# Decoder layer and gated cross attention: work beside the last cross group in other steps, and the mask of its last two batches on VectorE

## The chip, the cores and the metric

One Trainium2 chip; the kernel runs on one of its cores. The metric is the device time of one execution in microseconds (us). A core has TensorE (PE in the profile; PEld is its weight loads), VectorE (DVE), ScalarE (ACT), GpSimd (POOL) and SyncE (SP), which here issues nearly all DMAs.

## The reference, cut to what matters

All is float32: 16 batches of 128 tokens with 512 features, 16 heads of 32.

```python
# L0: a decoder layer
x = x + attention(layernorm(x), itself, ltor_mask) @ w_ao + b_ao            # A: self attention
x = x + attention(layernorm(x), ctx, cross_mask) @ w_co + b_co             # B: cross attention
x = x + gelu(layernorm(x) @ w1 + b1) @ w2 + b2                              # C: MLP, 512 -> 2048 -> 512
# attention: scores = q k^T / sqrt(32); scores = scores * mask - 10000 * (1 - mask); softmax; @ v
# L1: gated cross attention (D)
a = layernorm(ctx); scores = (x Wq^T)(a Wk^T)^T * scale, -inf where masked; softmax; @ (a Wv^T)
x = x + tanh(gate) * out @ Wo^T
```

The cross mask has a 128x128 plane of its own for each batch, shared by the heads.

## The kernel before

**Groups and sections.** The tokens stay in SBUF as four groups of four batches. `attend` (from line 651) runs sections A0 to A3, then B0 to B3 (B3 is "the last cross group"), then the MLP (`mlp`) for all groups, then the gated sections D0 to D3.

**Units and steps.** A section has 16 steps. Step k belongs to the unit (batch k // 4, quarter m = k % 4); a unit holds four heads' scores of one batch, 128 x 512. Scores of unit 2_1 are those of batch 2, quarter 1. One step issues, in this order: the four `pT` DMAs of a pair of units (`receive_pair`, at odd k - 5); the score matmuls of a whole batch at m = 0 (`sc_B`); the *jobs* planned for this step; the output product of a finished batch (`mo_B`); the product with the values at m == 2 of the batch that is two batches old (`mix`, `av_B`); `turn_unit` of unit k - 3 (VectorE transpose, then the DMA `away_B` to DRAM); `norm_unit` of unit k - 2 (VectorE reciprocal, POOL multiply `s_B<-s_B,sum_B`); `least_unit` and `exp_unit` of unit k - 1 (VectorE minimum `mn_B<-s_B`, ScalarE's four exps); `scale_unit` of this batch's units (VectorE, PSUM scores times the mask plane into SBUF: unit 0 in the first step, 1 and 2 in the second, 3 in the third); `add_mask` of this unit (POOL: s + ma, `s_B<-s_B,mask`). The trailing steps 16 to 23 of the last section drain the pipeline and have jobs too.

**Order.** Every instruction is issued through `InOrder`, which keeps each engine in program order (so all instructions have line 50 in the profile, and tiles are told apart by name). An engine that waits holds back all that is queued behind it. This goes for SP's queue of DMAs too.

**Jobs beside the last cross group.** `beside_last_cross` (line 1585) makes the plan. It has:
- `gated_start` (line 1349): keys and values of the first gated group from normalised encoder tokens (`key_job`, `value_job`: 8 matmuls each, `mm_v`, then a ScalarE copy and a DMA `kept_v_D`).
- `mlp_start` (line 1004): LayerNorm of the first MLP group's tokens, their way through DRAM (`turned_C`), the four returned parts (`ml.part`, DMA `back_C<-turned_C`) and `chunk_back`, which on ScalarE applies the LayerNorm's scale and bias (`T_C<-back_C`).
- `loads`: the steps in which one 256 KB block of the first weight tiles is sent for. w1_0, w1_1 and w2_0 (which of the two matrices, and the number of the hidden block) have four blocks each.
- `at_`: the steps in which the MLP's generator goes on to its next `yield`.

**The MLP.** Its products go by a scheme with 7 half-size products instead of 8. It needs sums of weight quarters (`weight_sums`, line 981: t1 to t4, `t<-w`) and of token quarters (`token_sums`: `sx`). For hidden block n, `sums` gives the sums for w1 (`t1_n`) and for w2 (`t2_n`). Those of w1_0 run on POOL, one for each of the generator's steps; those of w2_n and w1_(n+1) wait in a list, `todo`, and run on VectorE:

```python
for _ in range(min(2, len(todo))):      # line 1244, after each of the 7 products r
    todo.popleft()()
```

Each of the four sums of a weight tile subtracts two quarters; the first needs the tile's blocks 0 and 1, the second blocks 2 and 3 and the first sum. The products `h_0_p` of a hidden block (PSUM, PE) are then added up in SBUF by VectorE (`h<-h,h`); ScalarE applies GELU. The product `h_n_p` of the first block uses three PSUM tags in turn, those of later blocks one bank, `mm0`, which also held the last product of the first block.

**D's mask.** The gated sections set `adds_only`. There, VectorE adds a mask to each head's scores and finds the minimum in one custom instruction (`tensor_tensor_reduce`, `s_D<-sc_D,gmask`, 128x128 each, four to a unit with an accumulator read behind each), straight from PSUM.

Of the kernel before, what the change touches and what calls it, by code (L numbers as in the profile page):

```python
# [19 lines left out]
Q = 32  # L20
# [33 lines left out]
def decoder_then_gated_cross_attention(ctx: ExitStack, tc: tile.TileContext, a: dict, out: bass.AP):  # L54
# [451 lines left out]
    class Section:  # L506
# [1 line left out]

        deferred, v_bias, at_end, adds_only = False, None, False, False

        def mixed_tile(self, b):
            return work.tile([P, KC, S], F32, tag="mT", name=f"mT_{self.name}_{b}", bufs=1)
# [22 lines left out]
    def by_head(t):  # L537
        return t.rearrange("p n c j -> p c n j")

    def scale_unit(bt, j):  # L540
        s = work.tile([P, NQ, KC, Q], F32, tag="s", name=f"s_{bt.name}_{j}", bufs=7)
        if bt.by_array:
            s = s.rearrange("p n c j -> p (n c j)").rearrange("p (c n j) -> p n c j", c=KC, n=NQ)
        bt.s[j] = s
        sc = bt.sc.pop(j).rearrange("p (c n k) -> p c n k", c=KC, n=NQ)
        if bt.sec.adds_only:
            bt.mn[j] = least_tile(bt, j)
            bt.sec.mask_and_least(by_head(s), sc, bt.b, bt.mn[j])
        else:
            bt.sec.scale_mask(by_head(s), sc, bt.b)  # L550
# [2 lines left out]
        return work.tile([P, KC], F32, tag="mn", name=f"mn_{bt.name}_{j}", bufs=6)  # L553

    def least_unit(bt, j):
        if not bt.sec.adds_only:
            bt.mn[j] = least_tile(bt, j)
            nc.vector.tensor_reduce(bt.mn[j], by_head(bt.s[j]), AX.XY, ALU.min)

# [91 lines left out]
    def attend(sections, ready, others, after=None):  # L651

        if not ready:
            sections[0].start(sections[1])
        units, batches = [], []
        projected = deque()  # L660

        def by_transfer(n):

            return min(n, (len(sections) * GB - 1) * GB) if ready else n

        def step(k, bt=None, jobs=(), ahead=None):

            m = k % GB
            pair = k - 5
            if pair % 2 and 0 <= pair < by_transfer(len(units)):  # L670
                receive_pair(*units[pair])
            if m == 0 and bt is not None:
                scores(bt)
            due()
            for job in jobs:
                job()
            if projected and (m == 0 or ready and bt is None):
                before = projected.popleft()
                if before.sec.deferred:
                    afterwards("act", lambda: before.sec.put_away(before))  # L680
                else:
                    out_project(before)
            done = k // GB - 2
            if ready and k == by_transfer(k) + 7:
                done = len(batches) - 1
                mix(batches[done])
                projected.append(batches[done])
            elif m == 2 and 0 <= done < len(batches) - ready:
                mix(batches[done])
                projected.append(batches[done])  # L690
            if ahead is not None:
                ahead.prepare(k % NS)
            if 0 <= k - 3 < len(units):
                (turn_unit if k - 3 < by_transfer(k) else turn_by_array)(*units[k - 3])
            def norm():
                if 0 <= k - 2 < len(units):
                    norm_unit(*units[k - 2])

            def exp():
                if 0 <= k - 1 < len(units):  # L700
                    least_unit(*units[k - 1])
                    exp_unit(*units[k - 1])


            for do in (exp, norm) if ready else (norm, exp):
                do()
            if bt is not None:
                for j in SCALED[m]:
                    scale_unit(bt, j)
                bt.sec.add_mask(by_head(bt.s[m]), bt.b)  # L710

        k = 0
        for i, sec in enumerate(sections):
            last = i + 1 == len(sections)
            jobs = others() if last else sections[i + 1].jobs()
            ahead = sections[i + 2] if i + 2 < len(sections) else after if i + 2 == len(sections) else None
            for b in range(GB):
                bt = Batch(sec, b)
                batches.append(bt)
                for m in range(GB):  # L720
                    units.append((bt, m))
                    step(k, bt, jobs.get(k % NS, ()), ahead)
                    k += 1
        while projected or k < len(units) + 2 * GB:
            step(k, jobs=jobs.get(k - len(units) + NS, ()))
            k += 1
# [14 lines left out]
    class SelfAttention(Section):  # L741
# [107 lines left out]
        def add_mask(self, s, b):  # L849
            nc.gpsimd.tensor_tensor(s, s, bcast_rows(ma1), ALU.add)  # L850

    def encoder_rows(g):
        return a["ctx_2048"][g * GB : (g + 1) * GB].rearrange("b s d -> (b s) d")

# [18 lines left out]
    class CrossAttention(Section):  # L873
# [95 lines left out]
        def scale_mask(self, s, sc, b):  # L969
            nc.vector.tensor_tensor(s, sc, bcast_rows(self.ms[:, b, :]), ALU.mult)  # L970

        def add_mask(self, s, b):
            nc.gpsimd.tensor_tensor(s, s, bcast_rows(self.ma[:, b, :]), ALU.add)

# [29 lines left out]
    def mlp_start(ml):  # L1004

        ml.pieces = deque()

        ml.b2 = load_row(a["L0_xattn_b2"], "b2_row")
        ml.db1 = cpool.tile([P, NF], F32, tag="db1", name="db1")
        for i in range(NI):  # L1010
            b1, c0 = columns["b1"]
            c0 += i * KC
            nc.vector.tensor_tensor(
                ml.db1[:, 2 * i : 2 * i + 2], b1[:, c0 + 2 : c0 + 4], b1[:, c0 : c0 + 2], ALU.subtract
            )

        def row_difference():
            ml.db2 = work.tile([P, H], F32, tag="row", name="db2_row", bufs=2)
            nc.vector.tensor_tensor(ml.db2[:, 0:HF], ml.b2[:, HF:H], ml.b2[:, 0:HF], ALU.subtract)

        ml.lnT = []
        def start():
            ml.lnT.append(act_tile("C0"))
            ml_begin(0)

        sends = [lambda b=b: ml_send(0, b) for b in range(GB)]
        back = [lambda k=k: chunk_back(ml.lnT[0][:, k], ml.back, k, "ln3_s", "ln3_b") for k in range(KC)]
        return (
            ([start, row_difference, lambda: ml_receive(0)], [0, 5, 7]), (sends, [0, 1, 2, 3]), (back, [12, 13, 14, 15]),
            ([lambda m=m: ml.part(m) for m in range(NQ)], [7, 9, 9, 11])  # L1030
        )

    def ml_begin(g):
# [8 lines left out]
    def mlp(ml, last_steps):  # L1042
# [143 lines left out]
        O_ORDER = (0, 1, 3, 5, 6, 2, 4)  # L1186
        w1, w2, right1, right2 = {}, {}, {}, {}

        w1[0], w1[1], w2[0] = load(0, 1), load(1, 1), load(0, 2)
        yield  # L1190

        right1[0], todo, _ = sums(0, 1, "kT", w1.pop(0), nc.gpsimd)
# [8 lines left out]
        for n in range(len(steps) + 1):  # L1201
# [35 lines left out]
            for r in range(7):  # L1237
                if n < len(steps):
                    p = H_ORDER[r]
                    hidden_product(n, p, sides[p], right1[n][p], h)  # L1240
                if before is not None:
                    p = O_ORDER[r]
                    out_product(n - 1, p, before[0][p], right2[n - 1][p], acc)
                for _ in range(min(2, len(todo))):
                    todo.popleft()()
                for do in at_[r]:
                    if do is not None:
                        do()
                if r == 1 and n + 1 < len(steps):
                    w2[n + 1] = load(n + 1, 2)  # L1250
                elif r == 2 and n + 2 < len(steps):
                    w1[n + 2] = load(n + 2, 1)
                last_steps(n, r)
                if n == 1 and r == 3:
                    for d, t in unkept:
                        nc.sync.dma_start(out=d, in_=t)
                yield
# [91 lines left out]
    def gated_start(first):  # L1349
# [12 lines left out]
        def keep_later(key, t, n, wait):  # L1362
# [4 lines left out]

        return (
            ([lambda c=c: key_job(c) for c in range(KC)], [1, 2, 3, 5]),
            ([lambda b=b: value_job(b) for b in range(GB)], [7, 9, 11, 13]),  # L1370
        )

    class GatedAttention(Section):
# [184 lines left out]
                ([lambda g=g, b=b: send(g, b) for g in range(3) for b in range(GB)], [8, 9, 10, 11, 13, 14, 15, 16, 19, 19, 19, 19]),  # L1558
            )

        adds_only = True

        def mask_and_least(self, s, sc, b, least):

            ma = self.ma[:, b, :].rearrange("p (n k) -> p n k", k=Q)
            for c in range(KC):
                nc.vector.tensor_tensor_reduce(
                    s[:, c], sc[:, c], ma, 1.0, LARGEST, ALU.add, ALU.min, least[:, c : c + 1]
                )

        def add_mask(self, s, b):
            pass
# [12 lines left out]
    def beside_last_cross():  # L1585
        flip[0], in_blocks[0] = 2, False
        def piece():
            due()
            next(in_mlp)

        at_ = [0, 8, 10, 12, 14, 15, 15, 16, 16, 17, 18, 19, 19, 20, 21, 21, 22, 23, 23]
        loads = [3, 5, 5, 7, 11, 11, 13, 13, 14, 15, 15, 16]
        return plan(
            *gated_start(first), *mlp_start(ml), *decoder[-1].tokens_again([1, 1, 3], (1, 0, 2)), ([piece] * len(at_), at_),
            ([lambda: ml.pieces.popleft()()] * len(loads), loads),
        )
# [95 lines left out]
```

## Time and profile before

| | |
|---|---|
| median of 3 runs | 1166.15 us (1164.99 to 1167.93) |
| profiled execution | 1167.72 us, span 1165.9 us |
| granted TensorE clock, mean | 0.997 |
| PE busy | 1132.2 us, 97% of the span |
| VectorE, ScalarE, POOL busy | 739.5, 605.8, 701.3 us |
| HBM traffic | 164 MB read, 94 MB written, 222 GB/s |

"Busy" is the time in which the engine has an instruction running; PEclk is the granted clock in tenths of full speed. In a line of a timeline stand: start in us from the span's start, duration in us, engine, line, operation, out<-in with buffer numbers left out, shape, count, and in brackets the idle time of the engine before it and what ended that. An "SPq" line is SP's issuing of a DMA. The last cross group runs to about 530 us, the MLP follows from there.

### The profile page before, as it was taken

Reading aid. Unit: us, or ns where it says so; the run is one execution under the profiler, and the core shown is the slowest. Engines: PE = TensorE matmul, PEld = TensorE weight load, DVE = VectorE, ACT = ScalarE, POOL = GpSimd, SP = SyncE. Lnnn points to the kernel's source line nnn. Section 1 sums busy time; section 2 is a strip of 40 time slices with the busy share of each in tenths; the row PEclk is TensorE's granted clock in tenths of the full one; section 3 lists DMA queues with packets and bytes.
Section 4 is the critical chain, followed back from the end, with each engine's and each line's share of the span. In section 5 each row is a group of like instructions: output and inputs, shape, how many; then the busy total and the mean of one; then the engine's idle time right before and its main releaser. Section 6 shows DMA issues by size and latency. Waiting matters only on the chain. (4 is left out here: it accounts for less than half of the span.)

```text
span 1165.9 us, 22021 instructions
## 1 busy us (share of the span) xinstructions
PE 1132.2 (97%) x7202; PEld 862.6 (74%) x7202; DVE 739.5 (63%) x1893; ACT 605.8 (52%) x2132; POOL 701.3 (60%) x636
## 2 busy tenths in 40 slices
PE   6999999999999999998999999999999999999998
PEld 5877777657575756545788888888888777787875
DVE  7678878797878876866654634443441238767763
ACT  2467667666666766765231233223222247787653
POOL 7698878688868675675233514443342268454973
PEclk9999999999999999998999999999999999999999
DMA  6598979999889879898797696696447817988874
GB/s 228 148 221 223 239 187 221 249 243 261 196 227 213 235 203 248 240 283 256 258 299 235 181 293 187 201 276 253 154 160 240 245 48 200 255 239 236 262 213 158
DMA packets 325121, 259.78 MB, mean 223 GB/s; under 512 B 83528, under 2 KB 280336, under 8 KB 320144
## 3 DMA queue, kind: packets, MB, share of 16 engines
q1 hardware_dynamic: 324968, 258.38, 78.1%
q8 instruction: 57, 0.93, 0.3%
q14 instruction: 56, 0.46, 0.1%
q10 hardware_dynamic: 40, 0.01, 0.0%
HBM read 163.94 MB, written 94.37 MB: 222 GB/s over the span
## 5 line engine op out<-in xcount | busy, mean ns | idle before, releaser
L50 DVE TENSOR_TENSOR h<-h,h 128x512 f32<-128x512 f32 x80 | 54.9, 686 | 113.4 <-PE h L50 113.4
L50 ACT ACTIVATE s_A<-s_A,mn_A 128x128 f32<-128x128 f32 x256 | 99.5, 394 | 51.2 <-issue 37.3
L50 ACT ACTIVATE s_B<-s_B,mn_B 128x128 f32<-128x128 f32 x256 | 99.5, 393 | 47.0 <-issue 32.7
L50 ACT ACTIVATE h<-h 128x512 f32<-128x512 f32 x64 | 40.3, 630 | 160.6 <-DVE h L50 160.6
L50 POOL TENSOR_TENSOR s_D<-s_D,sum_D 128x512 f32<-128x512 f32 x64 | 66.6, 1041 | 63.4 <-DVE sum_D L50 60.1
L50 ACT ACTIVATE s_D<-s_D,mn_D 128x128 f32<-128x128 f32 x256 | 99.2, 392 | 0.1
L50 POOL TENSOR_TENSOR s_B<-s_B,sum_B 128x512 f32<-128x512 f32 x64 | 67.0, 1046 | 49.9 <-DVE sum_B L50 44.4
L50 POOL TENSOR_TENSOR s_A<-s_A,sum_A 128x512 f32<-128x512 f32 x64 | 66.5, 1040 | 36.0 <-DVE sum_A L50 35.5
L50 POOL TENSOR_TENSOR s_A<-s_A,ma 128x512 f32<-128x512 f32 x64 | 81.7, 1277 | 5.4 <-DVE s_A L50 3.7
L50 POOL TENSOR_TENSOR s_B<-s_B,mask 128x512 f32<-128x512 f32 x64 | 81.3, 1271 | 2.1 <-DMA away_B<-s_B 0.4
L50 POOL TENSOR_TENSOR rstd_aD<-rstd_aD,mhalf 128x1 f32<-128x1 f32 x12 | 6.6, 550 | 114.6 <-DVE rstd_aD L50 101.1
L50 POOL TENSOR_TENSOR sh<-h 128x512 f32<-128x512 f32 x32 | 40.7, 1272 | 51.0 <-ACT h L50 43.0
L50 PE MATMUL mo_B<-w_co,mT_B 128*128 128x512 f32 x128 | 60.9, 620 | 1.5 <-ACT mT_B L50 1.5
L50 PE MATMUL h<-T_C,t 128*128 128x256 f32 x256 | 60.7, 380 | 1.3 <-DVE h L50 1.3
L50 PE MATMUL h<-T_C,w 128*128 128x256 f32 x256 | 61.0, 381 | 0.8 <-DVE h L50 0.8
L50 PE MATMUL h<-sx,t 128*128 128x256 f32 x256 | 60.6, 379 | 0.0
L50 PE MATMUL o<-w,h 128*128 128x256 f32 x256 | 60.5, 379 | 0.0
L50 PE MATMUL o<-t,h 128*128 128x256 f32 x256 | 60.5, 379 | 0.0
L50 PE MATMUL o<-t,sh 128*128 128x256 f32 x256 | 60.5, 379 | 0.0
L50 PE MATMUL mo_A<-w_ao,mT_A 128*128 128x512 f32 x128 | 59.1, 604 | 0.0
L50 DVE CUSTOM_DVE_ANT_0 s_D<-sc_D,gmask 128x128 f32<-128x128 f32 x256 | 57.0, 283 | 1.0 <-DMA turned_x<-x_D 0.8
L50 PE MATMUL mm_q_B<-T_B,w_cq 128*128 128x512 f32 x128 | 57.3, 595 | 0.0
(324 smaller groups left out, 2977.5 us busy)
## 6 DMA issues: line engine op xcount, KB each, us to landing
t<-kept SPq DMA_DIRECT2D x24, 1024.0 KB, 7.6
away_A<-s_A SPq DMA_DIRECT2D x64, 256.0 KB, 2.8
pT_A<-away_A SPq DMA_DIRECT2D x128, 128.0 KB, 3.0
away_B<-s_B SPq DMA_DIRECT2D x64, 256.0 KB, 4.5
pT_B<-away_B SPq DMA_DIRECT2D x128, 128.0 KB, 3.6
away_D<-s_D SPq DMA_DIRECT2D x60, 256.0 KB, 3.9
pT_D<-away_D SPq DMA_DIRECT2D x120, 128.0 KB, 3.1
w<-in_L_xattn_w_dram SPq DMA_DIRECT2D x24, 512.0 KB, 5.8
```

The costliest lines, as they stand in the source:

```text
L50: return lambda *args, **kw: self.tc.keep_in_program_order(call(*args, **kw))
```

## The change

Five edits, all beside or in the last cross group and the first MLP hidden block.

1. Returned parts of the first MLP group are sent for in steps 7, 7, 9, 9 (before 7, 9, 9, 11), and `chunk_back` runs in steps 12, 13, 14, 14 (before 12 to 15).
2. The gated group's last two value jobs move from steps 11 and 13 to 13 and 15.
3. POOL's four sums of w1_0 go to steps 10, 11, 12, 13 (before 8, 10, 12, 14); the weight blocks after the first four are sent for in steps 13 to 18 (before 11 to 16), and w2_0 is loaded ahead of w1_1.
4. In hidden block 0, VectorE's weight sums run one behind each of products 0 to 3 and two behind 4 and 5 (before two behind each of 0 to 3).
5. In group B3, batches 2 and 3 (8 units): after the scale, VectorE adds the mask and finds the minimum with four custom instructions a unit, as in D but on the scaled scores in SBUF. POOL's `add_mask` and VectorE's `tensor_reduce` of those units go. `adds_only` becomes `by_head_from`, the batch from which a section does this: 0 in D, 2 in B3, never elsewhere.

```diff
 def scale_unit(bt, j):
-        if bt.sec.adds_only:
+        if bt.b >= bt.sec.by_head_from:
             bt.mn[j] = least_tile(bt, j)
             bt.sec.mask_and_least(by_head(s), sc, bt.b, bt.mn[j])
         else:
             bt.sec.scale_mask(by_head(s), sc, bt.b)
 def least_unit(bt, j):
-        if not bt.sec.adds_only:
+        if bt.b < bt.sec.by_head_from:
             bt.mn[j] = least_tile(bt, j)
             nc.vector.tensor_reduce(bt.mn[j], by_head(bt.s[j]), AX.XY, ALU.min)
 # attend.step
-                bt.sec.add_mask(by_head(bt.s[m]), bt.b)
+                if bt.b < sec.by_head_from:
+                    bt.sec.add_mask(by_head(bt.s[m]), bt.b)
+    def mask_by_head(s, sc, ma, least):
+        ma = ma.rearrange("p (n k) -> p n k", k=Q)
+        for c in range(KC):
+            nc.vector.tensor_tensor_reduce(
+                s[:, c], sc[:, c], ma, 1.0, LARGEST, ALU.add, ALU.min, least[:, c : c + 1]
+            )
 # CrossAttention
+        by_head_from = property(lambda self: 2 if self.g == NG - 1 else GB)
+        def mask_and_least(self, s, sc, b, least):
+            self.scale_mask(s, sc, b)
+            mask_by_head(s, s, self.ma[:, b, :], least)
 # mlp_start
-            ([start, row_difference, lambda: ml_receive(0)], [0, 5, 7]), (sends, [0, 1, 2, 3]), (back, [12, 13, 14, 15]),
-            ([lambda m=m: ml.part(m) for m in range(NQ)], [7, 9, 9, 11])
+            ([start, row_difference, lambda: ml_receive(0)], [0, 5, 7]), (sends, [0, 1, 2, 3]), (back, [12, 13, 14, 14]),
+            ([lambda m=m: ml.part(m) for m in range(NQ)], [7, 7, 9, 9])
 # mlp
-        w1[0], w1[1], w2[0] = load(0, 1), load(1, 1), load(0, 2)
+        w1[0], w2[0], w1[1] = load(0, 1), load(0, 2), load(1, 1)
-                for _ in range(min(2, len(todo))):
+                for _ in range(min(1 if n == 0 and r < GB else 2, len(todo))):
 # gated_start
-            ([lambda b=b: value_job(b) for b in range(GB)], [7, 9, 11, 13]),
+            ([lambda b=b: value_job(b) for b in range(GB)], [7, 9, 13, 15]),
 # beside_last_cross
-        at_ = [0, 8, 10, 12, 14, 15, 15, 16, 16, 17, 18, 19, 19, 20, 21, 21, 22, 23, 23]
-        loads = [3, 5, 5, 7, 11, 11, 13, 13, 14, 15, 15, 16]
+        at_ = [0, 10, 11, 12, 13, 15, 15, 16, 16, 17, 18, 19, 19, 20, 21, 21, 22, 23, 23]
+        loads = [3, 5, 5, 7, 13, 14, 15, 16, 17, 17, 18, 18]
```

More of the change, by code (lines that the diff above doesn't have):

```diff
@@ L506, in decoder_then_gated_cross_attention @@
     class Section:
-        deferred, v_bias, at_end, adds_only = False, None, False, False
+        deferred, v_bias, at_end, by_head_from = False, None, False, GB
         def mixed_tile(self, b):
@@ L1559, in deferred_jobs @@
             )
-        adds_only = True
+        by_head_from = 0
         def mask_and_least(self, s, sc, b, least):
[L1565 to L1569, printed above, removed]
+            mask_by_head(s, sc, self.ma[:, b, :], least)
         def add_mask(self, s, b):
```

## The prediction

> **What bounds the kernel now.** I read the page first. TensorE (PE) is busy 97% of the span and its clock is full except around one place, so only PE's idle time and its slow clock can be won, and any delay of PE is paid in full.
>
> ```profile
> PE 1132.2 (97%) x7202; PEld 862.6 (74%) x7202; DVE 739.5 (63%) x1893; ACT 605.8 (52%) x2132; POOL 701.3 (60%) x636
> PEclk9999999999999999998999999999999999999999
> ```
>
> The one slice with an 8 lies at 524 to 553 us: there the last cross group (B3) ends and the MLP begins, which is where the edit is. Then the windows of 5 us (the last three columns: granted clock, DMA share, GB/s):
>
> ```profile
> 520.00:525.00 5.00, 4.38 (x14) 1.66 (x12) 1.90 (x4) 2.97 (x10) 2.08 (x3) 1.00 1.08 289
> 525.00:530.00 5.00, 1.80 (x29) 1.38 (x29) 4.01 (x8) 4.84 (x21) 4.93 (x5) 0.70 0.92 259
> 530.00:535.00 5.00, 5.00 (x8) 2.22 (x9) 1.61 (x5) 2.99 (x12) 4.92 (x5) 0.62 1.01 300
> ```
>
> PE does little at 525 to 530 and runs at 0.62 to 0.70 of its clock to 535, while POOL is full. PE's timeline shows why, and what follows:
>
> ```profile
> 526.70 1.73 PE L50 MATMUL av_B<-pT_B,v_B 128*32 128x128 f32 x28 [2.32 <-DMA pT_B<-away_B]
> 529.92 5.59 PE L50 MATMUL mo_B<-w_co,mT_B 128*128 128x512 f32 x8 [1.50 <-ACT mT_B L50]
> 537.08 1.89 PE L50 MATMUL h<-sx,t 128*128 128x256 f32 x8
> 551.68 1.89 PE L50 MATMUL h<-sx,w 128*128 128x256 f32 x8
> 554.36 1.99 PE L50 MATMUL h<-T_C,w 128*128 128x256 f32 x8 [0.78 <-DVE h L50]
> ```
>
> Idle is 2.32 + 1.50 here and 2.42 in four smaller gaps to 575, 6.2 in all. The mo_B product of 5.59 takes 3.6 elsewhere and the av_B of 1.73 about .95: the slow clock costs 2.7. So the edit can win at most 8.9 us, and 6.5 of them sit at 524 to 535.
>
> **The change, part by part.** The order of every engine is fixed in the program, so I replayed the new order with the durations of these rows, start to start: scale .60, transpose .63, a weight sum or an h add .60 to .70 on VectorE (DVE); normalisation 1.00, mask add or sum 1.22 to 1.27 on POOL.
>
> *Token returns two steps earlier, loads of weight blocks later.* ScalarE's fourth T_C copy waited 2.98 us for a returned quarter, and DVE 2.46 and POOL 2.92 behind it. With the returns earlier and 768 KB of weight blocks no longer ahead, pT_1_3 lands at about 523.5 instead of 526.5, by some .9 us per 256 KB block. That wins up to the 6.5 us at 524 to 535, if nothing else is late next.
>
> *Value jobs in steps 13 and 15.* They are the same 2 x 8 matmuls of 3.6 us. Between the scores of batch 3 and the av of batch 1 they give PE work, and they queue nothing longer: nothing by themselves, as long as PE has work on either side.
>
> *POOL loses 8 mask adds:* 8 x 1.27 = 10.2 us of an engine that is full at 525 to 535. *DVE loses 8 reductions* (.57) *and gains 8 x 4 custom instructions with their accumulator reads.* In the gated section a unit of four takes .85 (1044.36 to 1045.21), so DVE gains 8 x (.85 - .57) = 2.3 us. But there the input is in PSUM, and here score and mask both lie in SBUF. Nothing of that form with POOL beside it is in this trace for custom instructions; for tensor_tensor it is:
>
> ```profile
> 609.70 1.64 DVE L50 TENSOR_TENSOR t<-w,t 128x512 f32<-128x512 f32 x1
> 611.26 1.75 DVE L50 TENSOR_TENSOR t<-w 128x512 f32<-128x512 f32 x1
> ```
>
> ```profile
> 609.07 1.72 POOL L50 TENSOR_TENSOR sx<-T_C 128x512 f32<-128x512 f32 x1
> 610.75 1.72 POOL L50 TENSOR_TENSOR sh<-h,sh 128x512 f32<-128x512 f32 x1
> ```
>
> The same sum takes .68 alone. Beside POOL each ends about when POOL's instruction ends: the two take turns whole. Instructions with an input in PSUM do not show it: the scale s_B<-sc_B takes .68 beside POOL too. [...]
>
> Taking the tensor_tensor rows as nearest (two SBUF inputs, same neighbour): units 2_1, 2_3 and 3_0 meet the rest of a normalisation (.62) and a sum that POOL starts straight after it (1.25 to 1.5), about 2.0 each; 3_1 meets .6; 3_3 meets a normalisation and two token sums, 3.15. The sum is 3 x 2.0 + .6 + 3.15 = 9.7 us of DVE waiting. Bounds: 0 (gated row) to 8 x 2 = 16.
>
> Does that matter? Up to the transpose of unit 3_2 (540.65), DVE idled 7.4 for POOL in nine waits, 2.46 for T_C and 2.77 for a w2_0 block, 12.7 in all. All of these can go; 9.7 + 2.3 = 12.0 come. In the replay this transpose stands at 540.5, so as before. Without the lock it stands at 533. PE: the scores of batch 3 wait for the bank that unit 2_3's scale frees, a gap of 2 to 3 at 512 to 515 that is new, and the MLP's second product waits for POOL's token sum until 537.55 against 537.08. So with the lock the 6.5 us at the front are spent before the MLP has begun: PE is .5 late, not early.
>
> *Weight loads and sums.* w2_0 is now loaded ahead of w1_1. Two blocks of w1_1 go in step 17, the last two in step 18. On SP's queue those stand behind away_3_2 (which waits for the transpose of 3_2), four pT_3_1 and the 1 MB of w2_1. Before, SP's timeline shows that place:
>
> ```profile
> 543.87 0.43 SPq L50 DMA_DIRECT2D w<-in_L_xattn_w_dram  x1
> 544.41 0.44 SPq L50 DMA_DIRECT2D away_B<-s_B  x1
> 544.89 0.51 SPq L50 DMA_DIRECT2D w<-in_L_xattn_w_dram  x1
> 552.97 1.75 SPq L50 DMA_DIRECT2D pT_B<-away_B  x4
> ```
>
> The first line is w2_1; the page of DMA issues there has 8.3 to its landing, so 552.2. The away_3_3 issued next landed at 552.9, and that is what the last line waited for. The blocks of w1_1 take the place of that away: issued at 544 to 544.7, landing at about 552.9 and 553.7 (range 551 to 555). DVE's queue now has, after the third h add at about 547, the second sum of w1_1, which needs them. Behind that sum stand five of what PE needs: two GELU-side h adds (1.42 together), x3 + mo_2 (.60), two sums (1.2), the adds h_0_3 and h_0_2 (1.35). Before, none of them waited for a block:
>
> ```profile
> 549.32 1.42 DVE L50 TENSOR_TENSOR h<-h 128x512 f32<-128x512 f32 x2 [0.96 <-ACT h L50]
> 553.61 0.69 DVE L50 TENSOR_TENSOR h<-h,h 128x512 f32<-128x512 f32 x1 [1.04 <-PE h L50]
> ```
>
> The next hidden block's first product (PE 554.36) needs the bank that the add at 553.61 frees. After: 553.7 + .6 + 1.42 + .60 + 1.2 + 1.35 = 558.9, less what overlaps: 558.8 against 554.36, +4.4. PE has no work of its own from about 553.6 on, a gap of 5 us. Bounds: landing at 551 gives +2, at 555 +5.7.
>
> *The clock.* The trace's rows: after the gap of 2.32 (with 1.73 of slim work and 1.50 more idle) the clock was 0.5 for 6.8 us; gaps of 2.15 and 1.74 elsewhere left it full. A gap of 5 us is beyond all of these. A 0.5 clock for 6.8 us of full work loses 3.4; nothing is the other end, and I take the middle, 1.7. [...]
>
> *The sums one per product (t2_0 at products 0 to 3, w1_1 at 4 and 5)* shift DVE work from ahead of the h adds to between them. Each h add comes up to .6 earlier; nothing of it is left behind the wait above.
>
> Sum: +4.4 (PE's delay at the next block holds the .5 of the front) + 1.7 = +6.1, and from there PE is bound (25.0 busy in 25 us), so it is kept to the end. The profiled execution took 1167.72 (span 1165.9 and 1.8 around it), 1.6 above the median of 1166.15; on that execution it gives 1173.8, on the median 1172.2. I say 1172.0. About 0.3%, or 3.5 us, is what a measurement can tell from no change.
>
> **The rivals.**
> *No lock, so faster (0.25).* The custom masks behave as in the gated section. The transpose of 3_2 comes at 533 and not 540.6, so w2_1 and the blocks are issued at some 537, and land at 546 to 547, when DVE gets there. The 6.5 us of the front are won and the next block's product starts at 547.6 to 551.2, 3.2 to 6.8 early: 1166.15 - 5 = 1161. For it: no custom row here shows a lock. Against: both inputs in SBUF, and POOL full of normalisations and token sums in that window. It decides if the units' customs take under .4 each beside POOL.
>
> *The lock holds, but the blocks land in time (0.19, no change).* DVE waits 5 to 6 us and not 9.7, because units and normalisations miss each other; the transpose comes at about 536, the blocks at 549, and the front's gain pays for the rest: 1163 to 1169. For it: DMA moved only 138 GB/s at 540 to 545. Against: three normalisations follow their unit's own scale at once.
>
> *The edit's gain is not where it is aimed (inside the forecast):* PE's new gap at 512 to 515, if it drops the clock there, adds up to 3.4: 1176.
>
> **How the numbers follow.** The forecast, lock and late blocks, gets 0.56: 1169 to 1177, by +2 to +5.7, 0 to 3.4 of clock and the gap at 512. No change: 0.19. Faster: 0.25, 1160 to 1162.6. The range runs from 1161 to 1177 and leaves some 0.1 on either side.
>
> **What would show it.** Right: the custom instructions on s_B in B3 at over .6 mean, DVE waiting 4 us or more for w at about 547 to 553, and PE waiting 3 us or more for DVE's h at the first product of the second hidden block. Wrong: custom instructions at .28, the transpose of 3_2 by 535, no wait for w in DVE's timeline past 545, and PE without idle time from 524 to 535 at clock 1.0.

## The result, and the profile after

The changed kernel takes 1171.40 us (median of 11 runs, 1167.86 to 1175.82); the kernel before, on the same chip, 1165.01 (1163.76 to 1167.93). The ratio is 1.0041, 95% interval 1.0025 to 1.0057: slower by 4.8 us. (The two medians lie 6.4 us apart, which the interval's 2.9 to 6.6 us still holds.) In a second series of runs it was 1.0031 (1.0019 to 1.0043), 3.6 us. The forecast was +6.

The page of the changed kernel: PE is busy 2.0 us longer than before, POOL 9.7 us shorter, VectorE 8.1 longer. The slow slice of TensorE's clock is gone from the row of slices, but not from the trace, as the windows below show.

```profile
span 1171.4 us, 22080 instructions
PE 1134.2 (97%) x7202; PEld 864.7 (74%) x7202; DVE 747.6 (64%) x1949; ACT 605.6 (52%) x2132; POOL 691.6 (59%) x628
PEclk9999999999999999999999999999999999999999
```

The windows show that the bad place has moved, not gone. At 525 to 535, PE is now busy 8.1 of 10 us (before 6.8) at full clock. Instead it is idle from 551.6 to 555.2, where before it worked, and the slow clock follows there:

```profile
525.00:530.00 5.00, 4.59 (x12) 1.85 (x11) 4.93 (x23) 5.00 (x20) 1.88 (x2) 1.00 0.81 241
530.00:535.00 5.00, 3.49 (x13) 1.98 (x11) 3.85 (x11) 3.28 (x15) 4.00 (x4) 1.00 0.76 240
550.00:555.00 5.00, 1.56 (x8) 1.03 (x6) 4.84 (x8) 1.05 (x2) 0.00 (x0) 1.00 1.04 322
555.00:560.00 5.00, 4.80 (x14) 3.90 (x15) 3.08 (x8) 2.35 (x5) 1.78 (x2) 0.66 0.88 244
```

PE's timeline, the same products as in the prediction (the last column is the idle time before, and what ended it):

```profile
528.06 3.70 PE L50 MATMUL mo_B<-w_co,mT_B 128*128 128x512 f32 x8 [0.41 <-ACT mT_B L50]
535.16 1.99 PE L50 MATMUL h<-sx,t 128*128 128x256 f32 x8 [1.67 <-POOL sx L50]
549.67 1.89 PE L50 MATMUL h<-sx,w 128*128 128x256 f32 x8
555.20 2.70 PE L50 MATMUL h<-T_C,w 128*128 128x256 f32 x8 [3.64 <-DVE h L50]
557.69 2.92 PE L50 MATMUL o<-w,h 128*128 128x256 f32 x8
```

The MLP's products come 1.9 us earlier than before (535.16 for 537.08) up to the end of the first hidden block. Then the second block's first product, 554.36 before, comes at 555.20, and from its start to that of the av_B product two products later it takes 5.34 us (to 560.54), where it took 3.65 before, since the clock is low (0.59 at 556 to 558, 0.56 at 558 to 560). The reason is one line of VectorE's timeline, the second sum of w1_1, which waits for the late block:

```profile
543.97 0.68 DVE L50 TENSOR_TENSOR t<-w 128x512 f32<-128x512 f32 x1
550.12 0.69 DVE L50 TENSOR_TENSOR t<-w,t 128x512 f32<-128x512 f32 x1 [5.47 <-DMA w<-in_L_xattn_w_dram]
550.73 1.41 DVE L50 TENSOR_TENSOR h<-h 128x512 f32<-128x512 f32 x2
552.06 0.68 DVE L50 TENSOR_TENSOR x<-x,mo_B 128x512 f32<-128x512 f32 x1
552.66 0.69 DVE L50 TENSOR_TENSOR t<-w 128x512 f32<-128x512 f32 x1
553.26 0.69 DVE L50 TENSOR_TENSOR t<-t,w 128x512 f32<-128x512 f32 x1
553.86 1.28 DVE L50 TENSOR_TENSOR h<-h,h 128x512 f32<-128x512 f32 x2
```

Behind the sum stand five more instructions, and then the two h adds of 553.86, of which the last frees the bank. On SP's timeline the three weight DMAs (w2_1 and the two blocks) are issued together, right behind the four `pT` DMAs, and the list of DMA issues has 6.6 us to the landing of the second block, issued at 543.41. The 256 KB away transfer issued at 532.73 took 2.6.

```profile
539.54 2.80 SPq L50 DMA_DIRECT2D pT_B<-away_B  x4
542.38 1.46 SPq L50 DMA_DIRECT2D w<-in_L_xattn_w_dram  x3
```

**The lock.** The prediction gives this name to the turns that VectorE and POOL take in its two pairs of rows at 609 to 613. VectorE's timeline of the changed kernel at unit 2_1, and POOL's beside it:

```profile
508.35 0.66 DVE L50 TENSOR_TENSOR s_B<-sc_B,mask 128x512 f32<-128x512 f32 x1
509.04 0.72 DVE L50 CUSTOM_DVE_ANT_0 s_B<-s_B,mask 128x128 f32<-128x128 f32 x1
509.69 1.34 DVE L50 CUSTOM_DVE_ANT_0 s_B<-s_B,mask 128x128 f32<-128x128 f32 x1
510.97 0.28 DVE L50 CUSTOM_DVE_ANT_0 s_B<-s_B,mask 128x128 f32<-128x128 f32 x1
```

```profile
508.58 1.04 POOL L50 TENSOR_TENSOR s_B<-s_B,sum_B 128x512 f32<-128x512 f32 x1 [3.68 <-DMA away_B<-s_B]
509.57 1.31 POOL L50 TENSOR_TENSOR t<-w 128x512 f32<-128x512 f32 x1
```

The first custom instruction ends 0.14 us after POOL's normalisation (509.76 for 509.62), the second 0.15 after POOL's sum (511.03 for 510.88). The third, with POOL idle, takes 0.28. The scale, whose scores come from PSUM, overlaps the normalisation and still takes 0.66.

### The profile page after: what moved, and what is told of

It reads as the page before. It is cut to its first block, busy times and chain, and to the rows that moved or that the text cites. A ratio compares the mean times of both kernels' runs of the same rounds, so it can differ in the third digit from the quotient of the medians.

```text
span 1171.4 us, 22080 instructions
## 1 busy us (share of the span) xinstructions
PE 1134.2 (97%) x7202; PEld 864.7 (74%) x7202; DVE 747.6 (64%) x1949; ACT 605.6 (52%) x2132; POOL 691.6 (59%) x628
## 5 line engine op out<-in xcount | busy, mean ns | idle before, releaser
L50 POOL TENSOR_TENSOR s_B<-s_B,mask 128x512 f32<-128x512 f32 x56 | 71.2, 1271 | 1.6
```

Source lines behind the costliest of these rows:

```text
L50: return lambda *args, **kw: self.tc.keep_in_program_order(call(*args, **kw))
```

## The experiments

Each was timed in five rounds beside the kernel before, on the same chip; ratios are to that. A single profile's span swings by several us in the gated sections, where every kernel here has the same instructions (the stretch from the MLP's second hidden block to the end took 605.6 to 613.7 us). So beside the ratio I give the *passage*: in the profile, from the start of the output product at 503.84 to that of the product `h<-sx,t` at 559.02, 55.18 us in the kernel before. It holds what the change moves on PE. Each passage is of one execution, the kernel before's too, and that need not be a typical one: e3's profile is of the fastest of its 12 runs (1165.00 us, median 1169.85), e11's of the slowest (1173.47, median 1169.88). Where passage and ratio differ, the ratio decides.

| kernel | ratio (95%) | passage, against before |
|---|---|---|
| changed | 1.0041 (1.0025 to 1.0057) | +3.0 |
| changed, again | 1.0031 (1.0019 to 1.0043) | +4.6 |
| e1 blocks early | 1.0004 (0.9993 to 1.0015) | -1.2 |
| e2 masks on POOL | 1.0022 (1.0008 to 1.0037) | +2.1 |
| e3 masks from PSUM | 1.0019 (1.0007 to 1.0031) | -1.2 |
| e4 masks on VectorE alone | 0.9997 (0.9985 to 1.0009) | -0.9 |
| e5 returned parts and value jobs alone | 1.0022 (1.0008 to 1.0036) | +1.8 |
| e6 loads and sums alone | 1.0027 (1.0012 to 1.0042) | +1.4 |
| e7 blocks early, masks on POOL | 0.9992 (0.9980 to 1.0004) | -0.5 |
| e8 blocks early, no lock | 0.9980 (0.9966 to 0.9995) | -3.6 |
| e9 as e8, last value job in step 13 | 1.0004 (0.9988 to 1.0020) | +2.8 |
| e10 masks alone, no lock | 1.0008 (0.9993 to 1.0023) | +0.9 |
| e11 returned parts alone | 1.0004 (0.9991 to 1.0017) | -0.1 |

**e1: the late block taken away.**

```diff
-        loads = [3, 5, 5, 7, 13, 14, 15, 16, 17, 17, 18, 18]
+        loads = [3, 5, 5, 7, 13, 14, 15, 16, 17, 17, 17, 17]
```

> The changed kernel with all four blocks of w1_1 sent for in step 17, so the last two no longer stand behind w2_1 on SP's queue. Theory (late block): VectorE's wait of 5.47 for w at 544.6 goes; the first product of the second hidden block, at 555.20 in the changed kernel, comes at about 552.3 behind PE's own work (549.67 + 1.89 + the 0.8 that the kernel before has there), the clock stays at 1.0 there (1.7 saved): 4 to 5 us less than the changed kernel, 1 to 3 less than the kernel before. Rival (the lock sets the end, the block only fills its shadow): the product moves by under 1 us and another wait ends there. Second rival: pT_3_1 or w2_1 come later by the time of two blocks, 1.8 us, and give it back within the next block.

VectorE's timeline has no wait for w left after 540, and PE's has

```profile
551.88 1.99 PE L50 MATMUL h<-T_C,w 128*128 128x256 f32 x8 [0.78 <-DVE h L50]
```

This is 3.3 us earlier than in the changed kernel, and at full clock (1.00 at 550 to 560). Two numbers in the step list are worth 0.37% (1.0004 against 1.0041), 4.3 us, as the theory said; against the second series of the changed kernel it is 0.27%. Against the kernel before it was to gain 1 to 3; the passage is 1.2 shorter, the timed runs show no difference.

**e2: masks of the last two batches back on POOL.**

```diff
-        by_head_from = property(lambda self: 2 if self.g == NG - 1 else GB)
+        by_head_from = GB
```

> The changed kernel with the mask of batches 2 and 3 of B3 back on POOL and the minimum as one reduction on VectorE; all other edits stay. Theory (the lock delays VectorE, that delays the transpose of unit 3_2, that delays the blocks): no custom instruction on s_B, but POOL has 10.2 us more, so POOL is full again and the token sums come late; the transpose of 3_2, 538.0 in the changed kernel, lies within 2 us of that, VectorE still waits 3 us or more for w, and the time is within 2 us of the changed kernel. Rival (the masks on VectorE are the whole loss): the transpose comes 4 us or more earlier and the time falls to that of the kernel before or below, 5 us or more.

The transpose of 3_2 came at 535.69 (538.02 in the changed kernel, so just outside the 2 us expected), and the late block is there all the same:

```profile
548.95 0.69 DVE L50 TENSOR_TENSOR t<-w,t 128x512 f32<-128x512 f32 x1 [5.49 <-DMA w<-in_L_xattn_w_dram]
```

PE waits 3.28 for VectorE and its clock drops to 0.55 at 554 to 556. The masks on VectorE are not what makes the block late. The ratio is 0.2% lower, but the intervals of the two kernels overlap, so what the masks cost in time is not shown here.

**e3: the custom instructions read PSUM.** The scale is lost in two batches; all else is the same.

```diff
             self.scale_mask(s, sc, b)
-            mask_by_head(s, s, self.ma[:, b, :], least)
+            mask_by_head(s, sc, self.ma[:, b, :], least)
```

> The changed kernel, but the 32 custom instructions of batches 2 and 3 in B3 read the scores from PSUM and write over the scaled ones, so that only the mask is an SBUF input (the scale by the mask plane is lost in those two batches; the number of instructions is the same). Theory (two SBUF inputs and POOL take turns whole): all of them take 0.28 to 0.30, VectorE's 7.6 us of excess in them goes, the transpose of 3_2 comes at 533 to 535 instead of 538.0, the blocks some 3 us earlier, and the time falls by 3 to 6 us. Rival (the custom instructions wait for something else, such as a value of POOL's or the accumulator): they still take up to 1.34 beside POOL, and the time stays.

The groups of the changed kernel and of e3 (minimum/median/maximum ns, first and last start):

```profile
L50 DVE CUSTOM_DVE_ANT_0 s_B<-s_B,mask x32: 277/289/1347, 504.9 to 530.7; 128x128 f32<-128x128 f32 x32
```

```profile
L50 DVE CUSTOM_DVE_ANT_0 s_B<-sc_B,mask x32: 285/286/292, 505.1 to 525.9; 128x128 f32<-128x128 f32 x32
```

All 32 fall to 0.29. Their sum goes from 16.6 to 9.2 us: 7.4 us of pure waiting, gone with the second SBUF input. The transpose of 3_2 comes at 533.4, the wait for w is 3.04 and the product at 552.82. PE now waits 1.84 for a pT_B transfer instead, and its clock falls behind that wait (1.78 us here for what takes 1.07 at full clock):

```profile
537.02 1.78 PE L50 MATMUL av_B<-pT_B,v_B 128*32 128x128 f32 x28 [1.84 <-DMA pT_B<-away_B]
```

In the timed runs it was worth 0.22%, 2.6 us, less than the 3 to 6 expected, and the intervals overlap. The passage is as short as e1's, but this is the execution of 1165.00, and the ratio still says slower.

**e4: edit 5 alone** (edits 1 to 4 as in the kernel before).

> The kernel before with edit 5 alone: VectorE masks batches 2 and 3 of B3, nothing else is moved. Theory: the custom instructions are held by POOL's normalisations and sums for 5 to 9 us in all, but POOL's 10.2 us fewer and the waits for POOL that go (7.4) pay for most of it, and w1_1's blocks are early here: no wait for w beyond that of w2_0; PE's 6.5 us at 524 to 535 stay, since they are set by the returned parts and the loads. Time within 2 us of the kernel before. Rival (the lock itself makes the kernel slower): 3 us or more slower than before, with PE's idle time before 535 grown by that. Second rival (the masks on VectorE are the gain of the edit): 3 us or more faster.

The custom instructions take 16.7 us here too, and the time is that of the kernel before. PE's idle time is elsewhere, not less: 1.91 for mT_B, 2.05 for the token sum, 1.34 for pT_B. So edit 5 does not by itself make the kernel slower, lock included.

**The changed kernel again.** Same program.

> The changed kernel once more, for a second profile. Theory: the late block is in the schedule, so VectorE's wait for w near 544.6 (5.47 in the first profile) and PE's idle time ahead of the second hidden block (3.64) are there again within 1.5 us; the wait of 2.98 for a pT_D pair at 1034 in the gated sections is an accident of one execution and is under 1.5 this time. Rival: the change moves the gated sections' transfers as well, and the wait at 1034 is there again. Time 0.2 to 0.6 per cent above the kernel before.

```profile
556.24 3.78 PE L50 MATMUL h<-T_C,w 128*128 128x256 f32 x8 [4.66 <-DVE h L50]
1033.80 1.07 PE L50 MATMUL av_D<-pT_D,v_D 128*32 128x128 f32 x28 [1.13 <-DMA pT_D<-away_D]
```

The wait for w is 6.39 and PE's 4.66, and the second block took 7.6 us to land: the late block belongs to the schedule. The wait in the gated section was 2.98 in the first profile and is 1.13 here. So of the 5.5 us between the first two spans, 3.0 are the change's passage; 3.0 came behind it (609.8 against 606.9 us to the end), 0.5 was won ahead of it, and behind it the second execution lost nothing (606.3).

**e5: edits 1 and 2 alone.**

> The kernel before with edits 1 and 2 alone: returned parts two steps earlier, last value jobs in steps 13 and 15; masks, loads and sums as before. Theory: ScalarE's wait of 2.98 for a returned part goes, PE has a value job between the product with the values of batch 1 and its output product, so the 1.50 for mT_B goes and the clock stays up (2.7 with it); the wait for pT_1_3 (2.32) is met 3.6 us earlier by PE and grows or a scale's bank is waited for at 512. 1 to 4 us less than the kernel before at the second hidden block's first product. Rival: POOL is full at 525 to 535 anyway and gives the gain back before the token sums, 0 at that product.

Neither theory nor rival: slower by 2.6 us. PE's timeline:

```profile
526.88 1.14 PE L50 MATMUL av_B<-pT_B,v_B 128*32 128x128 f32 x28 [2.88 <-DMA pT_B<-away_B]
```

PE gets to this product with one value job fewer ahead of it, pT_1_3 still has the old loads of weight blocks in front of it on the queue, and the clock falls to 0.50 at 528 to 530. But the kernel before loses as much here: the first MLP product comes 31.4 us after the passage's start, 31.5 before. What is longer is the next wait for a pT_B transfer, 0.31 in the kernel before:

```profile
542.11 1.07 PE L50 MATMUL av_B<-pT_B,v_B 128*32 128x128 f32 x28 [1.65 <-DMA pT_B<-away_B]
```

**e6: edits 3 and 4 alone.**

> The kernel before with edits 3 and 4 alone: weight blocks later and w2_0 ahead of w1_1, POOL's sums in steps 10 to 13, VectorE's sums one by one; masks on POOL, returned parts and value jobs as before. Theory (late block): the last two blocks of w1_1 stand behind w2_1, VectorE waits 4 us or more for w, PE idles 3 us or more ahead of the second hidden block and its clock drops: 2 to 6 us slower than the kernel before. Rival (the block is late only because edits 1, 2 and 5 hasten VectorE or delay the transpose): under 2 us of wait for w, time within 2 us of before.

```profile
549.36 0.69 DVE L50 TENSOR_TENSOR t<-w,t 128x512 f32<-128x512 f32 x1 [4.49 <-DMA w<-in_L_xattn_w_dram]
```

```profile
554.44 3.42 PE L50 MATMUL h<-T_C,w 128*128 128x256 f32 x8 [2.28 <-DVE h L50]
```

The late block is there without any of the other edits: 4.49 us of wait, 2.28 idle on PE (3 or more was expected), 3.42 for a product of 1.99. 3.2 us slower, within what the theory gave. The passage is only 1.4 longer, and all of that is the slow clock behind the gap (0.71 at 554 to 556, 0.50 at 556 to 558): this product starts 50.2 us after the passage's start, 50.5 in the kernel before. Ahead of the MLP, PE waits 3.98 for mT_B here, in place of the 2.32 + 1.50 before:

```profile
529.16 6.27 PE L50 MATMUL mo_B<-w_co,mT_B 128*128 128x512 f32 x8 [3.98 <-ACT mT_B L50]
```

**e7: e1 and e2 together.**

> The changed kernel with all blocks of w1_1 in step 17 and the masks of batches 2 and 3 back on POOL: edits 1 to 4 without the late block and without the lock. Theory: no wait for w, the transpose of 3_2 at about 536 as with the masks on POOL, first product of the second hidden block at 551 to 552 (the kernel before 554.36): 2 to 3 us less than the kernel before, if the gated sections give nothing back. Rival (the gain at the second hidden block isn't kept to the end): the same time as before, though that product comes 2 us early.

There is no wait for the blocks of w1_1, but PE waits 0.99, 2.36 and 1.96 for pT_B, and the product comes 0.5 earlier by the passage, not 2 to 3: the `pT` transfers that the products with the values need are what PE waits for instead. The timed runs show no difference to the kernel before.

**e8: neither the late block nor the lock.** Nothing is left out: the scaled scores go back to PSUM, and the custom instructions read them from there.

```diff
-        loads = [3, 5, 5, 7, 13, 14, 15, 16, 17, 17, 18, 18]
+        loads = [3, 5, 5, 7, 13, 14, 15, 16, 17, 17, 17, 17]
-            self.scale_mask(s, sc, b)
-            mask_by_head(s, s, self.ma[:, b, :], least)
+            self.scale_mask(sc, sc, b)
+            mask_by_head(s, sc, self.ma[:, b, :], least)
```

> The changed kernel with all blocks of w1_1 in step 17, and the scale of batches 2 and 3 in B3 written back over the scores in PSUM, so that the custom instructions have one input in PSUM and one in SBUF: nothing is left out, the same number of instructions, neither the late block nor the lock. Theory: custom instructions at 0.28 to 0.30, no wait for w, the token sums and the transpose of 3_2 earlier, the first product of the second hidden block at about 551.5 against 554.36 before and 551.88 with the lock: 1 to 3 us less than the kernel before. Rival (what stays at 505 to 540 are waits for pT transfers and for the token sum, which neither touches): the same as with the blocks early alone, ratio 0.999 to 1.001. Second rival: a scale that writes PSUM takes over 0.8 or holds the score bank, and PE's wait at 513 grows past 2.

```profile
525.00:530.00 5.00, 5.00 (x13) 2.28 (x12) 2.60 (x12) 5.00 (x21) 4.92 (x5) 1.00 0.87 259
530.00:535.00 5.00, 5.00 (x22) 3.44 (x20) 2.54 (x6) 2.91 (x14) 3.57 (x4) 1.00 1.00 279
```

```profile
550.53 2.00 PE L50 MATMUL h<-T_C,w 128*128 128x256 f32 x8 [0.78 <-DVE h L50]
```

The windows that were the worst of the kernel before are full, at full clock. The custom instructions take 0.285 to 0.292 here too, though they read what the scale has just written: the changed kernel's did not wait for the scale. The ratio of 0.9980 is the only one below 1 by its interval (1166.58 against 1168.49) and the lowest of all, but the intervals of e4 and e7 overlap it. From e1 to e8 the lock is worth 2.4 us of passage, and 0.24% in the timed runs, with intervals that just touch.

**e9: e8 with the last value job in step 13.**

> As the run before, with the last value job in step 13 and not 15, so that both value jobs stand ahead of the product with the values of batch 1. Theory (PE comes to that product before pT_1_3 has landed): its wait, 0.2 to 2.4 in the kernels with the job in step 15, is under 0.3, and the wait of the output product of batch 1 for mT_B, 0.2 to 0.4 there, is back at 1.5 to 2.0: within 1.5 us of the run before. Rival (the clock drops again at 526 to 534): 2 to 3 us slower.

```profile
532.17 6.46 PE L50 MATMUL mo_B<-w_co,mT_B 128*128 128x512 f32 x8 [4.42 <-ACT mT_B L50]
```

The wait for pT_1_3 is gone, but that for mT_B grows to 4.42 and the clock falls to 0.59 at 530 to 535: the rival. The timed difference to e8 is 0.24%, with intervals that overlap a little. The passage is 6.3 us longer, but not all of that is this wait: in this execution the clock was also low at 514 to 519, where e8's was full (the score product at 513.50 and the output product behind it took 1.70 and 4.76, in e8 1.12 and 3.70). The value job between the two products is what covers ScalarE's copy in e8 (no such wait there).

**e10: edit 5 alone, through PSUM.**

> The kernel before with edit 5 alone, the scaled scores written back to PSUM as above: the masks on VectorE without the lock and with no step moved. Theory: with the lock this edit alone gave 0.9997 and PE waited 2.05 for a token sum, 1.34 for pT_B and 1.91 for mT_B; without it the token sum's wait goes and the ratio is 0.997 to 0.999. Rival (the lock lies beside slack): 0.9995 to 1.0005 as with the lock.

```profile
540.04 1.69 PE L50 MATMUL av_B<-pT_B,v_B 128*32 128x128 f32 x28 [4.32 <-DMA pT_B<-away_B]
```

A miss: 1.0008, no gain. The wait for the token sum went as expected, and PE waited 4.32 for a pT_B transfer instead. The transfer was hardly later than in the kernel before (the product starts at 540.04, there at 539.62); PE came to it 3.6 us earlier (at 535.72, there at 539.31). What the masks won ahead of it was waited for here, and the clock fell to 0.58 behind the wait.

**e11: edit 1 alone.**

> The kernel before with edit 1 alone: returned parts in steps 7, 7, 9, 9, copies in 12, 13, 14, 14. Edits 1 and 2 together gave 1.0022, with a wait of 2.88 for pT_B at 526.9. Theory (the value jobs' shift is what costs: PE reaches the product with the values of batch 1 3.6 us sooner and finds no pT_1_3): alone, the returned parts win, 0.998 to 1.000, ScalarE's wait of 2.98 is under 1. Rival (the returned parts cost, as they stand ahead of the away and pT transfers on the queue): 1.001 to 1.003 alone too.

ScalarE's wait for the returned part is gone, and nothing is won: mT_B is now waited for 2.58 us, and the clock falls behind that wait (0.80 at 525 to 530, 0.86 at 530 to 535). 1.0004 lies between the two expectations, and its interval overlaps that of e5; that the value jobs are what costs in e5 is likely, not shown.

## Why the prediction was right

The direction and the mechanism held: late block, VectorE blocked in front of the h adds, PE idle ahead of the second hidden block, slow clock behind it. The size held in the timed runs, but some of its terms were too large, and one was a middle of bounds. Step by step:

- *The lock.* Predicted 9.7 us of waiting and custom instructions at over 0.6 mean; measured 7.4 and 0.52 (16.6 over 32). The units met POOL as listed, but 2_1, 2_3 and 3_0 lost 1.4 to 1.7 each and not 2.0, 3_1 0.4, and 3_3 2.5 and not 3.15. e3 and e8 show the cause: an SBUF input less, and all waiting goes. Up to 1.35 for one with two SBUF inputs (the changed kernel), 0.285 to 0.292 with one. The units that found POOL idle, 2_0, 2_2 and 3_2, took 0.28 to 0.29 with two as well. One reading of the prediction was loose: its two tensor_tensor rows end 0.55 after POOL's instruction, not with it. They run behind it.
- *The front, mis-sized by 2.4 us.* The prediction spent all of the 6.5 us before the MLP and had PE 0.5 late at the product at 537.08. It was 1.9 early. The transpose of 3_2 came at 538.0, not 540.5, and the token sum 2.4 earlier, mostly since the lock was smaller. The new gap for the bank of 2_3's scale, put at 2 to 3, was 1.33; another 0.83 just ahead of it was a wait for a pT_B transfer. The clock stayed full (1.00 from 500 to 555). The 0.9 us for a 256 KB block was an estimate; the 289 GB/s of 520 to 525 before give as much.
- *The late block: right, its landing put too late by 3.7 us.* Landing was put at 553.7 from the away transfer of before. The issue came 1.1 to 1.3 us earlier (542.9 and 543.4), and from there the second block took 6.6, so it landed at 550.0. VectorE was blocked 5.47 from 544.6, and the chain behind it took 5.0 (5.2 in the sum). So the product came +0.84 (in the second profile +1.88) and not +4.4. e1 shows that this block carries the loss: taken away, 1.0041 becomes 1.0004. e6 shows that it is late without edits 1, 2 and 5 (1.0027). It is not all that can cost: edits 1 and 2 alone gave 1.0022 (e5), and why that does not add up in the changed kernel is not shown. Nor did a run separate the 1 MB ahead of the blocks from the four `pT` DMAs behind which they are issued.
- *The clock: right.* 1.7 predicted, 1.7 measured from 555.20 to the av_B product (lag +0.84 to +2.53), and 2.3 in the second profile. But 1.7 was the middle between nothing and 3.4, so to hit it was luck.
- *"Value jobs: nothing by themselves": wrong.* They cover mT_B where pT_1_3 is on time: without the one in step 15 that wait is 4.42 (e9).
- *Sum.* +4.4 + 1.7 against +0.84 + 1.7 at the same place. That is 2.5, and 4.2 in the second execution; the whole passage lost 3.0 and 4.6, and the timed runs 3.6 to 4.8. All of it is below the 6.1, since the lock and the landing were both charged too much.

The rival "no lock, so faster" was half right about what would follow: without the lock but with the block late (e3), the kernel is still slower, and without the lock but with nothing moved (e10) it is the same; only early blocks and no lock together (e8) win.

## What to carry to other kernels

When a load is moved later, look up what stands before it in its queue at the new place, and what stands behind its first reader on that reader's engine: two 256 KB blocks one step later, behind four other DMAs and 1 MB, cost more than the four other edits together could win (1.0041 with them late, 1.0004 in e1). Before moving an elementwise operation to VectorE beside a busy POOL, count its SBUF inputs: 32 custom instructions took 16.6 us with two here, and 9.2 with one (e3). A step that left its result in PSUM avoided the waiting at no cost in instructions (e8: 0.285 to 0.292 each, and 0.68 for the scale as before). And judge a passage of a long kernel by the stretch of trace that holds it, as well as by the total, which has its own swing elsewhere; but by more than one execution of each, since e3's passage was short where its timed runs were slow.

## What the runs showed of the hardware that was not expected

TensorE's clock fell after idle gaps of well under 3 us, and no one length of gap decided it. From 500 us on, the clock fell behind each of the ten gaps of 2.58 us (e11) to 4.66 (the changed kernel, again): to 0.50 to 0.59 in the windows read behind seven of them, and behind e6's 3.98 and e11's 2.58 the output product took 6.27 and 5.25 for 3.60, behind e11's 2.92 the one with the values 1.92 for 1.07. From 2.15 to 2.44 both happened: the clock fell after 2.28 and 2.30 (e6), 2.32 (before), 2.36 (e7) and 2.40 (e2), and stayed full after 2.18 (e8), 2.40 (e7) and 2.44 (e9), all three at 1026 to 1034. One gap is the same in seven profiles, 2.15 us ahead of `mm_o_D` at 1125 to 1131: the clock fell behind it in e5 and e11, and stayed full in the kernel before, both executions of the changed kernel, e6 and e7. The same product took 1.99 us in the changed kernel and 3.58 in e11:

```profile
1130.73 1.99 PE L50 MATMUL mm_o_D<-gsums_o,mixed 128*128 128x256 f32 x8 [2.15 <-DVE x L50]
1128.54 3.58 PE L50 MATMUL mm_o_D<-gsums_o,mixed 128*128 128x256 f32 x8 [2.15 <-DVE x L50]
```

The clock fell after shorter waits too: after 1.84 in e3 at 537 (1.78 us for a product of 1.07), and after 1.02 and 0.64 close together in e9 at 510 to 514 (1.70 for 1.12). So an estimate of what such a gap costs has to allow for both outcomes, and this is one part of the swing between the executions here: in the gated sections, which have the same instructions in every kernel, that one product differs by 1.59 us.

The fall came while TensorE was still idle, or after it had started again. In the changed kernel the windows show 1.00 through the idle stretch at 552 to 554 and 0.59 at 556 to 558. In its second execution, the third line, the clock was down to 0.54 at 554 to 556, with no product running.

```profile
552.00:554.00 2.00, 0.00 (x0) 0.00 (x0) 2.00 (x5) 0.63 (x1) 0.00 (x0) 1.00 1.12 283
556.00:558.00 2.00, 2.00 (x7) 1.64 (x6) 1.41 (x4) 0.06 (x1) 0.44 (x1) 0.59 0.98 303
554.00:556.00 2.00, 0.00 (x0) 0.00 (x0) 2.00 (x4) 0.38 (x1) 0.00 (x0) 0.54 0.72 211
```
